# A decoder layer on one core: low halves of the weights from ACT and an accumulating DMA

## The chip, the core and the metric

The kernel runs on one core of a Trainium2 chip. The core has a matrix engine (TensorE: PE for its matmuls, PEld for its weight loads), a vector engine (VectorE: DVE), a scalar engine (ScalarE: ACT), a general engine (GpSimd: POOL), an engine for synchronisation (SyncE: SP), and 16 DMA engines. Each engine has its own queue of instructions and works through it in order; between engines there are semaphores. Matmuls write to PSUM, of which this kernel uses eight banks; all else on chip lies in SBUF.

The metric is the device time of one execution in microseconds (us), the median of the runs.

## What is computed

One layer of a decoder, for 8 batches of 100 tokens of width 1024, in float32: a retention over the own tokens, an attention over 722 context tokens and the own ones, and a gated feed-forward, each followed by a residual sum and a layer norm.

```python
x = _layernorm(x + _L0_attn_ref(x, Wq, Wk, Wv, Wg, Wo, g_norm_weight))
x = _layernorm(x + _L0_xattn_ref(x, ctx_2048, wq, wk, wv, wo, wk_ctx, wv_ctx, q_norm_w, k_norm_w))
x = _layernorm(x + _L0_ffn_ref(x, w_gate, w_up, w_down))

# _L0_attn_ref: 8 heads, keys of 128, values of 256
q, k, v, g = hidden @ Wq, hidden @ Wk, hidden @ Wv, hidden @ Wg        # q and k then with rotary factors
scores = einsum('bihd,bjhd->bhij', q * scale, k) * D[None]             # D: decay, causal
o = einsum('bhij,bjhd->bihd', scores, v)
o = o * rsqrt(mean(o * o) + EPS) * g_norm_weight * (g * sigmoid(g))
return o.reshape(B, T, H * DV) @ Wo

# _L0_xattn_ref: 16 heads of 128, 4 kv heads
q, k, v = x @ wq, x @ wk, x @ wv                                       # q, k normed, then rotary factors
# keys and values of the context in front of the own ones, softmax, then @ wo

# _L0_ffn_ref
return (silu(x @ w_gate.T) * (x @ w_up.T)) @ w_down.T
```

## The kernel before

**Products.** A product in float32 is made of three fast passes. Each operand is split into a high half, which is the operand rounded to the 12 significant bits that one pass takes, and a low half, which is what is left: `split2` (L68 to L70) does it with a copy by ACT into the type float32r (L69, CAST in the profile) and a subtraction by DVE (L70). `mm3` (L87 to L90) then issues three matmuls of 128 x 128 weights on 400 tokens: high by high, high by low, low by high. So nearly all of PE's work stands on L88, L89 and L90.

**Weights.** `load_w` (L72) loads a block of weights [128, 1024] (8 k tiles of 128 x 128, 512 KB) into one of three staging buffers `wst` by a DMA that SP issues (L78), and splits it into one of four buffers `w`. One such block gives 24 matmuls for each half of the tokens. A staging buffer may be loaded again when DVE's subtraction has read it; a buffer `w` may be written again when PE is done with it.

**Stages.** The tokens are worked on in two halves of 4 batches (400 tokens).

1. Retention (first attention), head by head: projections, scores, o, gate; the result goes to DRAM (`o1d`).
2. `out_proj` (L208) with `wo1`, for each half: loads the half's o from DRAM into four tiles `big` (L387 in `load_o1`), then for eight blocks of rows and two parts of the 2048 rows of weights, `load_w(w[m, c])` (L220) and 24 matmuls; adds the residual `rs` (L228, L231), and norms the half (`norm_root`, `norm_early`, `norm_late`, `scaled`; the result is stored to `zd`, L265). The four tiles of one half take the place of those of the other half.
3. Queries, keys and values of the own tokens for the second attention, called here the second retention projections (the loop over `kv`): for each of 4 kv heads six blocks of weights (four of queries, one of keys, one of values), in groups of two (four and two for the first head), `ws = [load_w(w2[kv, i]) ...]`, each used for both halves. Of each product of q or k, ACT makes the squares (L414), POOL sums them over the partitions (`partition_all_reduce`, L125), ACT and DVE make the inverse root (`inv_root`, L112 to L120), DVE applies the rotary factors to PSUM (`rope`, L134 to L137) and the root (L419), ACT and DVE split the result `d`, and SP stores it (`qd`, `kd`, L423; `vd`, L411). The bank of PSUM is free when rope has read it.
4. Second attention, per batch and kv head, with context projections, scores, softmax (two more `partition_all_reduce`, `mb`) and o (`o2d`).
5. `out_proj` with `wo2`, again for two halves.
6. Feed-forward, by seven instead of eight products of blocks.

**Order.** The tile framework orders the instructions of each engine by a model of their times and puts in the semaphores; buffers of a pool are taken in turn, and a writer waits for the last reader of its buffer. So the order on each queue follows from the program and that model, not from the text alone.

**What the change touches.** `load_w` as called in `out_proj` (64 blocks: 2 halves x 8 x 2, in two stages) and in the loop over `kv` (24 blocks). The names above are those of the profile's lines: `w<-wst` is the split of a block of weights, `wst<-in_wo` the load of a block of Wo or wo, `wst<-in_w` that of the other weights, `ss<-sq` the all-reduce of the squares, `big<-o1d` and `big<-o2d` the loads of o.

Of the kernel before, what the change touches and what calls it, by code (L numbers as in the profile page):

```python
# [8 lines left out]
F32 = mybir.dt.float32  # L9
FR = mybir.dt.float32r  # L10
AF = mybir.ActivationFunctionType
ALU = mybir.AluOpType
# [4 lines left out]
P = 128  # L17
B, T, D = 8, 100, 1024
NB = 4                 # batches in a half
N = NB * T             # tokens in a half  # L20
KT = D // P            # k tiles of the model width
QT = KT // 2           # k tiles in one of the four big tiles
SC, SH = 722, 362      # context tokens per batch, and in the first half of it
SN = [SH, SC - SH]
NC = 7                 # chunks of keys: SC of the context, then T own ones
ORDER = (6, 5, 0, 1, 2, 3, 4)
C5 = SC - 5 * P        # context keys in chunk 5
R6 = SC + T - 6 * P    # keys in chunk 6
T6 = T - R6            # first token that sees keys of chunk 6
N6 = 4 * R6            # scores of chunk 6, of the tokens that see its keys  # L30
NH1 = 8                # heads of the first attention
NKV = 4                # kv heads of the second
NHID = 32              # blocks of the hidden width
UNITS = NHID // 2      # pairs of hidden blocks
LAST = 3               # pairs of the last down projection
CUT = 5 * T            # tokens in the first of the two parts that are normed last
# [5 lines left out]
def decoder_layer(ctx, tc, xT, cT, w1, wo1, w2, wo2, wc, w3, wd, gw, qw, kw, trig, dec, mask, out):  # L42
# [21 lines left out]
    def split(dst, src):  # L64
        """dst[:, 0] + dst[:, 1] == src, each with the 12 significant bits that one pass takes."""
        split2(dst[:, 0], dst[:, 1], src)
# [5 lines left out]
    def load_w(src, w=None, parts=1):  # L72
        st = wp.tile([P, KT * P], F32, tag="wst", name="wst", bufs=3)
        if w is None:
            w = wp.tile([P, 2, KT * P], FR, tag="w", name="w", bufs=4)
        for i in range(parts):
            c = slice(i * KT * P // parts, (i + 1) * KT * P // parts)
            nc.sync.dma_start(out=st[:, c], in_=src[:, c])  # L78
            split(w[:, :, c], st[:, c])
        return w  # L80
# [30 lines left out]

    def inv_root(pool, ss, eps, n=N):  # L112
        """-2 (ss + eps)^-1/2: by exp(-ln/2), then a Newton step."""
        r = pool.tile([P, n], F32, tag="r0", name="r0")
        nc.scalar.activation(r, ss, AF.Ln, bias=eps)  # L115
        nc.scalar.activation(r, r, AF.Exp, scale=-0.5)  # L116
        q = pool.tile([P, n], F32, tag="r1", name="r1")
        nc.scalar.activation(q, r, AF.Square)
        nc.vector.scalar_tensor_tensor(q, ss, eps, q, ALU.add, ALU.mult)  # L119
        nc.vector.scalar_tensor_tensor(q, q, 3.0, r, ALU.subtract, ALU.mult)  # L120
        return q
# [6 lines left out]
    def rope(pool, acc, cosw, sinw, tag="t1"):  # L128
        """acc * cos + (acc with its halves swapped) * sin."""
        t1 = pool.tile([P, N], F32, tag=tag, name=tag)  # L130
        t2 = pool.tile([P, N], F32, tag="t2", name="t2")
        a = bt(acc)
        h = P // 2
        nc.vector.tensor_tensor(bt(t1), a, cosw[:, None, :].to_broadcast([P, NB, T]), ALU.mult)  # L134
        nc.vector.tensor_tensor(bt(t2[0:h]), a[h:P], sinw[h:P, None, :].to_broadcast([h, NB, T]), ALU.mult)
        nc.vector.tensor_tensor(bt(t2[h:P]), a[0:h], sinw[0:h, None, :].to_broadcast([h, NB, T]), ALU.mult)  # L136
        nc.vector.tensor_tensor(t1, t1, t2, ALU.add)  # L137
        return t1

    def tokens_first(pool, acc):  # L140
        """[128, 4 x 100] -> PSUM [100, 4 x 128]: the transposes of the four batches."""
        vt = pool.tile([P, N], F32, tag="vt", name="vt", bufs=1)
        nc.scalar.copy(vt, acc)
        tr = bank("s")
        for b in range(NB):
            nc.tensor.transpose(tr[0:T, b * P:(b + 1) * P], vt[:, b * T:(b + 1) * T], ident)
        return tr[0:T]

# [1 line left out]
    o1d = dr.tile([NH1, P, 2, 2, 2, N], FR, name="o1d")            # head, p, half, block, hi/lo, token  # L150
# [42 lines left out]
    def load_constants(p, trg):  # L193
        dcy = p.tile([T, NH1, T], F32, name="dcy", bufs=1)
        nc.sync.dma_start(out=dcy, in_=dec)
        nc.sync.dma_start(out=msk, in_=mask)
        nc.sync.dma_start(out=wts[:, 0:2], in_=gw)
        nc.sync.dma_start(out=wts[:, 2:3], in_=qw)
        nc.sync.dma_start(out=wts[:, 3:4], in_=kw)
        # rotary tables with the norm weights of q and k; factors left over from inv_root  # L200
        nc.vector.tensor_scalar(gws, wts[:, 0:2], -8.0, None, ALU.mult)
        nc.vector.tensor_scalar(kws, wts[:, 3:4], -0.5 * math.sqrt(P), None, ALU.mult)
        nc.vector.tensor_scalar(tq, trg[:, 2:4], wts[:, 2:3], None, ALU.mult)
        nc.vector.tensor_scalar(tk, trg[:, 2:4], wts[:, 3:4], None, ALU.mult)
        return dcy

# [1 line left out]
    def out_proj(half, w, load_o, res, yp, ybufs, p, make_z, dst, after=None):  # L208
        """res + o @ w of one half, then its layer norm: split for the next products, and to dst."""
# [4 lines left out]
        for ms in [range(first)] + [[m] for m in range(first, KT)]:  # L214
# [3 lines left out]
            for c in range(2):  # L218
                for m, acc in zip(ms, accs):
                    wt = load_w(w[m, c])  # L220
                    for k in range(KT):
                        kt = c * KT + k
                        rh, rl = og(kt)
                        a = acc if len(rh.shape) == 2 else bt(acc)
                        mmw(a, wt, k, rh, rl, kt == 0, kt == 2 * KT - 1)
# [55 lines left out]
    # A norm with little left to do once the last block of rows is there: all blocks are taken relative to the mean  # L281
    # of the others, so that the mean of what they then hold, delta, is that of the last block alone, and the
    # variance is mean(y^2) - delta^2 (delta^2 is at most an eighth of mean(y^2)).
# [24 lines left out]
    with sbuf("l1", 2) as p:  # L308
# [17 lines left out]
        for h in range(NH1):  # L326
# [14 lines left out]
            # scores with their decay, and o^T  # L341
# [21 lines left out]
            # a block of the context weights, split once for all batches  # L363
# [33 lines left out]
    kapool = sbuf("ka", 2, "right")  # L397
    ka = kapool.__enter__()
    with sbuf("l2", 2) as p:
        for kv in range(NKV):  # L400
            for i0, i1 in ((0, 4), (4, 6)) if kv == 0 else ((0, 2), (2, 4), (4, 6)):
                ws = [load_w(w2[kv, i]) for i in range(i0, i1)]
# [24 lines left out]
    y2pool = sbuf("y2", 1)  # L427
    y2p = y2pool.__enter__()
    with sbuf("cx", 2) as p, sbuf("c1", 1) as p1:
        for b in range(B):  # L430
# [10 lines left out]
            for kv in range(NKV):  # L441
                # K^T of the context, to be scaled by its norms when the scores leave PSUM, and V
# [29 lines left out]
                # -2 / norm of the context keys, keys on partitions  # L472
# [14 lines left out]
                # scores, keys on partitions, and their maximum  # L487
# [23 lines left out]
                # exponentials, split, and their sum  # L511
# [27 lines left out]
                # 1 / sum: exp(-ln), then a Newton step (the sum is 1 or more)  # L539
# [22 lines left out]
    # [C11 C12; C21 C22] = [A11 A12; A21 A22] [B11 B12; B21 B22] by Strassen's seven products; the rows of A  # L562
    # are two blocks of one weight, the columns of B the two halves of the tokens
# [60 lines left out]
    def w_pair(*ops):  # L624
        """Two of the sums of quarters of a weight, split; a sum goes to the first quarter's place unless that is kept."""
# [15 lines left out]
    def seven(i, part, t0=None):  # L641
        """Two blocks of the gate (part 0) or of the other factor (part 1): C11, C12, C21, C22."""
# [19 lines left out]
        def add(t, x, y, op=ALU.add):  # L662
            nc.vector.tensor_tensor(t, x, y, op)  # L663
# [3 lines left out]
        add(s2, s2, s4)                                     # C21  # L667
# [6 lines left out]
        add(s4, s4, prod(t2, 1, "b11+b12"))                 # C22  # L674
        m5 = prod(t3, 0, "b22")
        add(s1, s1, m5, ALU.subtract)                       # C11
        add(s3, s3, m5)                                     # C12
        return s1, s3, s2, s4

    # the first two blocks by all eight products: half of them need the first half of the tokens alone  # L680
# [13 lines left out]
    with sbuf("ff", 1) as p:  # L694
# [59 lines left out]
        # the last rows are normed in two parts  # L754
# [16 lines left out]
def _chunks(w, n):  # L771
    """[K, M] -> [M / 128, K / (n 128), 128, n 128]: k tiles of 128 x 128 side by side."""
    import numpy as np
    K, M = w.shape
    a = w.reshape(K // (n * P), n, P, M // P, P)
    return np.ascontiguousarray(a.transpose(3, 0, 2, 1, 4)).reshape(M // P, K // (n * P), P, n * P)
# [62 lines left out]
```

## Time and profile before

| | us |
|---|---|
| median of 3 runs | 2617.55 |
| lowest and highest of them | 2616.77, 2619.95 |
| span of the profiled execution | 2615.0 |
| PE busy in it | 2552.7 |
| DVE busy | 1922.2 |
| ACT busy | 1256.3 |
| POOL busy | 466.3 |

The span runs from the first to the last instruction of one execution that the hardware profiler recorded; the median of the runs is 2.55 us above it. A matmul's record of some 340 ns overlaps the next one's; at full clock they start 0.18 us apart. The page's map of the span, in 40 slices of 65 us, has the busy share of a slice in tenths, the granted clock of PE and the share of the 16 DMA engines:

```profile
PE   8999999999998899999999999999999999999998
...
DVE  4454554456999888888988989866866766866885
ACT  4555544533555455655655566533433433423351
POOL 0010000000544434434333343100000000000000
PEclk9999999999999999999999999999999999999999
DMA  5323333664434644544554553564421211211221
```

The first out_proj is in slices 8 to 10 (counted from 1), the second retention projections in 11 to 14, the second out_proj in 26 to 28. In a row such as `L70 DVE TENSOR_TENSOR w<-wst,w 128x1024 ... x300 | 303.7, 1015` the numbers after the bar are the busy time of the group and the mean nanoseconds of one. In a list of waits, `PE a L88 <- DVE t L136: 22.9, 5, 7.1` says that PE, at matmuls of L88 into banks `a`, waited for DVE's instruction of L136, 22.9 us in total, five times, at most 7.1 us.

### The profile page before, as it was taken

The page shows a single profiled execution, that of the slowest core. Times are in us where ns is not written, and L with a number is a line of the kernel's source. Part 1 is how long each engine was busy: PE and PEld are TensorE (multiplying, and loading weights), DVE is VectorE, ACT ScalarE, POOL GpSimd, SP SyncE. Part 2 cuts the span into 40 slices and gives each one's busy share as a digit, 9 for nine tenths or more (in the row PEclk, how much of TensorE's full clock was granted, in tenths as well). Part 3 has the DMA queues.
Part 4 walks back from the last instruction along what each step waited for, and adds up shares of the span by engine and source line. Part 5 has one row for each costly group of instructions (what it writes and reads, how often), then busy time and mean ns, then how long its engine had stood idle before and what let it go on. Part 6 is the DMA issues. An engine that isn't in the chain of part 4 may idle for free.

```text
span 2615.0 us, 37589 instructions
## 1 busy us (share of the span) xinstructions
PE 2552.7 (98%) x14438; PEld 2511.4 (96%) x14438; DVE 1922.2 (74%) x3201; ACT 1256.3 (48%) x2202; POOL 466.3 (18%) x222
## 2 busy tenths in 40 slices
PE   8999999999998899999999999999999999999998
PEld 8999999999998899999999999999999999999996
DVE  4454554456999888888988989866866766866885
ACT  4555544533555455655655566533433433423351
POOL 0010000000544434434333343100000000000000
PEclk9999999999999999999999999999999999999999
DMA  5323333664434644544554553564421211211221
GB/s 173 98 98 119 100 117 122 214 241 154 144 133 138 236 158 137 188 158 146 174 166 139 185 173 113 210 245 143 146 73 65 73 57 65 81 50 64 70 84 51
DMA packets 157233, 346.44 MB, mean 132 GB/s; under 512 B 45018, under 2 KB 95578, under 8 KB 147838
## 3 DMA queue, kind: packets, MB, share of 16 engines
q1 hardware_dynamic: 157054, 344.05, 39.5%
q8 instruction: 113, 1.85, 0.3%
q14 instruction: 66, 0.54, 0.1%
HBM read 279.81 MB, written 64.19 MB: 132 GB/s over the span
## 4 chain that ended last, share of the span: by engine, by line
PE 80%; DVE 10%; ACT 6%; issue 3%; DMA 2%; SPq 0%; DVEq 0%; ACTq 0%
PE a L88 16%; PE a L90 16%; PE a L89 16%; PE s L88 8%; PE s L89 8%; PE s L90 8%; PE v L88 3%; PE v L90 2%; PE v L89 2%; DVE r L119 1%; ACT L116 1%; ACT L115 1%; PE s L469 1%; DVE ot L378 1%; DVE t L136 1%
## 5 line engine op out<-in xcount | busy, mean ns | idle before, releaser
L88 PE MATMUL a<-big,w 128*128 128x400 f32 (+2 forms) x2300 | 778.5, 339 | 17.1 <-ACT big L69 9.5
L89 PE MATMUL a<-big,w 128*128 128x400 f32 (+2 forms) x2300 | 779.7, 339 | 0.0
L90 PE MATMUL a<-big,w 128*128 128x400 f32 (+2 forms) x2300 | 778.3, 339 | 0.0
L88 PEld LDWEIGHTS a<-big,w 128*128 128x128 f32 x2300 | 432.4, 188 | 20.6 <-ACT big L69 9.8
L90 PEld LDWEIGHTS a<-big,w 128*128 128x128 f32 x2300 | 433.9, 189 | 0.6
L89 PEld LDWEIGHTS a<-big,w 128*128 128x128 f32 x2300 | 433.1, 188 | 1.1 <-DVE big L70 0.5
L69 ACT CAST w<-wst 128x1024 fp32r<-128x1024 f32 (+2 forms) x300 | 259.2, 869 | 346.6 <-PE a L90 152.6
L70 DVE TENSOR_TENSOR w<-wst,w 128x1024 fp32r<-128x1024 f32 (+2 forms) x300 | 303.7, 1015 | 164.8 <-ACT w L69 163.2
L125 POOL PARTITION_ALL_REDUCE ss<-sq x56 | 157.3, 2817 | 725.4 <-DVE sq L362 442.3
L459 POOL PARTITION_ALL_REDUCE kss<-ksq x64 | 171.6, 2682 | 141.2 <-ACT ksq L458 140.7
L69 ACT CAST w<-as 128x512 fp32r<-128x512 f32 x90 | 55.9, 621 | 215.3 <-PE a L90 180.9
L88 PE MATMUL s<-big,w 128*128 128x400 f32 x428 | 150.4, 352 | 2.5 <-ACT big L69 2.5
L89 PE MATMUL s<-big,w 128*128 128x400 f32 x428 | 149.4, 349 | 1.6 <-DVE big L70 1.6
L90 PE MATMUL s<-big,w 128*128 128x400 f32 x428 | 148.8, 348 | 0.0
L505 ACT ACTIVATE s<-s,rk 128x400 f32<-128x400 f32 x160 | 88.0, 591 | 97.3 <-DVE sm L527 63.3
L663 DVE TENSOR_TENSOR s<-s 128x400 f32<-128x400 f32 x183 | 102.4, 569 | 25.3 <-ACT s L659 19.5
L125 POOL PARTITION_ALL_REDUCE mb<-sm x32 | 83.3, 2603 | 201.1 <-DVE sm L527 201.1
L524 ACT ACTIVATE s<-s 128x800 f32<-128x800 f32 (+1 forms) x128 | 95.1, 750 | 41.0 <-DVE s L518 38.1
L70 DVE TENSOR_TENSOR pl<-s,ph 128x800 fp32r<-128x800 f32 (+1 forms) x128 | 108.3, 850 | 2.5 <-ACT ph L69 2.0
L506 DVE TENSOR_TENSOR mx<-mx,s 128x400 f32<-128x400 f32 x128 | 80.5, 629 | 26.5 <-ACT s L505 23.3
L88 PE MATMUL a<-z,w 128*128 128x400 f32 x192 | 70.5, 367 | 24.0 <-DVE t L136 22.9
L69 ACT CAST ph<-s 128x800 fp32r<-128x800 f32 (+1 forms) x128 | 92.4, 731 | 0.9
(269 smaller groups left out, 5605.6 us busy)
## 6 DMA issues: line engine op xcount, KB each, us to landing
wst<-in_w SPq DMA_DIRECT2D x137, 512.0 KB
w<-wcd SPq DMA_DIRECT2D x64, 1024.0 KB
wst<-in_wo SPq DMA_DIRECT2D x64, 512.0 KB
wst<-in_wd SPq DMA_DIRECT2D x32, 512.0 KB
o1d<-of SPq DMA_DIRECT2D x32, 400.0 KB
big<-o1d SPq DMA_DIRECT2D x16, 800.0 KB
qd<-d SPq DMA_DIRECT2D x32, 400.0 KB
q<-qd SPq DMA_DIRECT2D x32, 400.0 KB
```

The costliest lines, as they stand in the source:

```text
L69: nc.scalar.copy(hi, src)
L70: nc.vector.tensor_tensor(lo, src, f32(hi), ALU.subtract)
L88: nc.tensor.matmul(acc, lh, rh, start=start, stop=False)
L89: nc.tensor.matmul(acc, lh, rl, start=False, stop=False)
L90: nc.tensor.matmul(acc, ll, rh, start=False, stop=stop)
L115: nc.scalar.activation(r, ss, AF.Ln, bias=eps)
L125: nc.gpsimd.partition_all_reduce(y, x, P, op)
L459: nc.gpsimd.partition_all_reduce(ss[:, at], sq[:, at], P, RED.add)
L505: nc.scalar.activation(sc, sp, AF.Copy, scale=rk[:, c:c + 1])
L506: nc.vector.tensor_tensor(mx, s[:, 1] if j == 2 else mx, sc, ALU.max)
L524: nc.scalar.activation(e, e, AF.Exp)
L663: nc.vector.tensor_tensor(t, x, y, op)
```

## The change

A second loader, `load_wa`, takes the place of `load_w` in `out_proj` and in the loop over `kv`. SP loads the staging buffer as before, and ACT makes the high half. Then ACT writes the negated high half where the low half is to be, and a DMA issued by POOL adds the staging buffer to it: low = -high + weight. DVE has no part in it. `load_w` stays for all other weights. The rest of the diff takes out comments and docstrings; the new function moves the lines behind it down by ten.

```diff
+    def load_wa(src):
+
+        st = wp.tile([P, KT * P], F32, tag="wst", name="wst", bufs=3)
+        w = wp.tile([P, 2, KT * P], FR, tag="w", name="w", bufs=4)
+        nc.sync.dma_start(out=st, in_=src)
+        nc.scalar.copy(w[:, 0], st)
+        nc.scalar.activation(w[:, 1], f32(w[:, 0]), AF.Copy, scale=-1.0)
+        nc.gpsimd.dma_start(out=f32(w[:, 1]), in_=st, accum_op=ALU.add)
+        return w
+
...
     def out_proj(half, w, load_o, res, yp, ybufs, p, make_z, dst, after=None):
...
-                    wt = load_w(w[m, c])
+                    wt = load_wa(w[m, c])
...
         for kv in range(NKV):
             for i0, i1 in ((0, 4), (4, 6)) if kv == 0 else ((0, 2), (2, 4), (4, 6)):
-                ws = [load_w(w2[kv, i]) for i in range(i0, i1)]
+                ws = [load_wa(w2[kv, i]) for i in range(i0, i1)]
```

## The prediction

> **What bounds the kernel now.** I read the page's engine rows first, then PE's waits stage by stage, then the stretches of time in which the changed loads stand. PE is the bound almost everywhere.
>
> ```profile
> span 2615.0 us, 37589 instructions
> PE 2552.7 (98%) x14438; PEld 2511.4 (96%) x14438; DVE 1922.2 (74%) x3201; ACT 1256.3 (48%) x2202; POOL 466.3 (18%) x222
> ```
>
> So only what makes PE wait counts. The first out_proj begins near 505 us, the second retention projections run from about 655 to 875, and the second out_proj from about 1685 to 1820. PE's waits from 500 to 880 us:
>
> ```profile
> PE a L88 <- DVE t L136: 22.9, 5, 7.1
> PE s L270 <- DVE s L245: 1.4, 1, 1.4
> PE a L88 <- ACT w L69: 1.1, 1, 1.1
> ...
> ```
>
> The reader is to see that DVE holds PE for 22.9 us in all, always by rope's last read of a PSUM bank (L136). Five stretches of that stage, then four of the two out_proj stages (us; busy PE, PEld, DVE, ACT, POOL; granted clock; DMA share; GB/s):
>
> ```profile
> 680.00:710.00 30.00, 25.26 (x127) 24.52 (x126) 29.62 (x53) 16.91 (x33) 14.92 (x6) 0.89 0.40 135
> 710.00:740.00 30.00, 30.00 (x167) 30.00 (x166) 29.52 (x44) 15.79 (x31) 16.12 (x6) 1.00 0.38 135
> 740.00:770.00 30.00, 27.36 (x146) 26.91 (x145) 29.71 (x47) 16.79 (x32) 11.37 (x5) 0.94 0.37 125
> 800.00:830.00 30.00, 22.94 (x115) 22.46 (x114) 29.61 (x46) 15.97 (x30) 12.52 (x5) 0.83 0.39 134
> 870.00:886.00 16.00, 9.20 (x39) 9.12 (x40) 14.84 (x29) 8.56 (x18) 7.81 (x3) 0.79 0.38 147
> ...
> 510.00:520.00 10.00, 9.88 (x55) 9.54 (x55) 2.45 (x2) 2.54 (x3) 0.00 (x0) 1.00 0.98 350
> 525.00:555.00 30.00, 30.00 (x168) 30.00 (x167) 12.86 (x16) 7.36 (x7) 0.00 (x0) 1.00 0.51 165
> 565.00:580.00 15.00, 13.63 (x74) 13.30 (x74) 12.40 (x20) 7.08 (x11) 0.00 (x0) 1.00 1.02 416
> 1730.00:1748.00 18.00, 16.72 (x88) 16.09 (x88) 13.64 (x21) 7.12 (x12) 0.00 (x0) 1.00 1.03 407
> ```
>
> In the projections DVE is full (29.5 to 29.7 of 30 us), and after each wait the granted clock falls too. In out_proj it is the reverse: DVE is under half busy in 525 to 555 and PE loses nothing there, but the DMA engines are full at the start of the stage (0.98) and where one half's o gives way to the other's (1.02, 1.03). Two more views: ACT and SP in time order.
>
> ```profile
> 512.77 1.05 ACT L69 CAST w<-wst 128x1024 fp32r<-128x1024 f32 x1 [1.98 <-DMA wst<-in_wo]
> 519.31 1.05 ACT L69 CAST w<-wst 128x1024 fp32r<-128x1024 f32 x1 [5.49 <-DMA wst<-in_wo]
> 521.64 1.05 ACT L69 CAST w<-wst 128x1024 fp32r<-128x1024 f32 x1 [1.29 <-PE a L90]
> 525.99 1.05 ACT L69 CAST w<-wst 128x1024 fp32r<-128x1024 f32 x1 [3.30 <-PE a L90]
> ```
> ```profile
> 509.44 2.97 SPq L78 DMA_DIRECT2D wst<-in_wo  x2
> ...
> 528.34 0.33 SPq L78 DMA_DIRECT2D wst<-in_wo  x1
> ```
>
> A weight lasts PE 4.35 us (521.64 to 525.99). The load issued at 509.44 was used at 512.77: 3.3 us. Its successor, issued at 512.08, was used at 519.31: 7.2 us, in the full stretch. The cast of 525.99 lets wst be loaded again at 528.34, 2.35 us later.
>
> **The change, part by part.** 88 weights change: 2 halves x 8 x 2 in each out_proj (64) and 4 x 6 in the projections.
>
> *Taken from DVE:* 88 subtractions (L70, 128x1024). Their groups by stage have 1221 ns in out_proj and 1443 ns in the projections: 64 x 1.22 + 24 x 1.44 = 113 us. In out_proj that is idle time of DVE made longer, worth nothing: PE covers it there. In the projections it is 35 us of a full engine. What PE loses there, against the 167 matmuls of the undisturbed row, clock included: (167-127) + (167-146) + (167-115) matmuls of 0.18 us, and 50 in 870 to 886 (89 fit into 16 us): 7.2 + 3.8 + 9.4 + 9.0 = 29 us. That is the ceiling of the gain. Its floor is zero, as these weights now come later and may be waited for instead of DVE. I take 12: the new way of a weight goes through POOL, whose queue in this stage also has 40 all-reduces of 2.85 us and waits for ACT and DVE in turn.
>
> *Added to ACT:* 88 negations of 128x1024. The cast of this size has 1.05 us; 92 us in all. ACT's rows (7.4 of 30, 17 of 30 us) hide them; each is 1.05 us on the way of its weight.
>
> *Added to POOL:* 88 DMA issues, in order with the all-reduces. In the changed order two stand ahead of the last head's two all-reduces, 20 between those of the projections, 10 among the last softmax reductions. Each waits for its negation, and that for PE to release a w buffer; behind it stand all-reduces whose results ACT (L115) and then DVE (L119) wait for. No POOL DMA is in the trace: the price of an issue lies between SP's 0.33 us and the 2.85 us of an all-reduce. I take 0.33, as the same kind of row; 24 of them are 8 us of a stage in which POOL is idle half the time, nothing on the path. At 2.85 they would fill 68 us of it and eat the gain of 12.
>
> *Added to the DMA engines:* 88 moves of 512 KB that read two operands and write one. At the full rows' 416 GB/s one pass of 512 KB keeps all engines for 1.27 us. Bounds: one pass (1.27, as a plain copy) and three (3.8: read, read, write each at full price); I take two (2.54), both reads passing where one did. In the even part of out_proj the engines are busy 0.51 x 4.35 = 2.2 us per weight; with 2.54 that is 4.75 against PE's 4.35, an excess of 0.4; by the 0.45 share of another even stretch (610 to 628 us), 0.15. Of the 64 weights some 48 lie in such stretches: 7 to 19 us, I take 13. The other 16 lie in the full stretches, four to five in each of 510-520, 565-580 and 1730-1748 with what leads to them: 4.6 x 2.54 = 12 us of transfers with no room, beside the o1d and o2d tiles that PE needs next. Some of it falls behind the need, but a PE wait here brings the slow clock too (0.83 above): I take 10 us for each, 30 (bounds: 0, as landings may have slack, and 17 each at three passes).
>
> *Moved on SP:* the reload of wst waited for DVE's subtraction, 2.35 us after the cast began; now for the accumulating DMA: 1.05 + 1.05 + 0.33 + 3.3 (the load's own time) + 1.27 (second pass) = 7.0 us. With the load itself 10.3 us for three wst buffers that must turn round in 3 x 4.35 = 13.0 us: it holds in the even part, and not with a load of 7.2 us. Behind the waiting reload on SP stand rs, the o tiles and zd. At the change of halves the new order has two wst loads ahead of the eight zd stores, not three, and those stores wait for the norm; so one weight less is in hand there. Price 0 (if the buffers in hand cover it) to 10 us (a load's 3.3, two ACT passes, the accumulation's 4.9, for each half change); I take 5 for each out_proj, 10.
>
> *The Trainium skill.* "DMA: Bandwidth & Descriptors", "Issuing engines are not separate DMA queues", says that DMAs issued from several engines run on the same 16 DMA engines and interleave. That speaks against this change; the rows at 1.02 show these engines full, and if POOL's were separate, the 13 and 30 would vanish and the time be about 2616. The same page ("Anatomy of one DMA — SWDGE (gpsimd) path") fits a POOL DMA as 2.0 us + bytes / 436e3 per us: 3.2 us for 512 KB, an estimate that knows no second read; by it the round of wst is 9.0 us, and only the 10 would shrink. No row here shows a POOL DMA.
>
> **Sum** against the profiled execution: 2615.0 - 12 + 13 + 30 + 10 = 2656. The median of the runs is 2617.55, 2.55 above that span, so 2658.6; I say **2658**. With the bounds that stay at two passes (gain 29 to 0, even part 7 to 19, full stretches 15 to 36, SP 0 to 20) it is 2611 to 2692.
>
> **Rivals.**
> 1. *The accumulation is dearer (three passes, 3.8 us).* Then out_proj is DMA-bound throughout: 2.2 + 3.8 = 6.0 us per weight, 1.65 over PE's, x 48 = 79; the full stretches 3 x 17 = 51; no gain in the projections: 2617.55 + 130 = 2748. For it: there is no spare time at 1.02. Against it: reads and the write may overlap.
> 2. *Faster: DVE's relief decides.* If an accumulation costs one pass, the even part needs 2.2 + 1.27 = 3.5 of 4.35 us and stays hidden, and the tiles' landings have slack. Then the gain of the projections stands nearly alone, 22 of the 29 less 7 at the full stretches: 2603. It decides as soon as an accumulation takes under about 2 us of the engines. For it: DVE is full where PE waits. Against: the row at 510 us, in which PE already loses 0.12 us for a late o tile.
> 3. *Gain and loss cancel.* One pass, with 12 us gained and as much lost at the stretches: 2617. That the change does not do what it says is excluded: in the changed order DVE has no w subtraction left in these stages.
>
> **How the numbers follow.** Chances: the forecast 0.60, rival 1 0.22, rival 2 0.09, rival 3 0.09. What can be told from no change is 0.2%, 5 us. Faster 0.09, same 0.09, slower 0.82. The range takes in rival 3 and the lower part of rival 1 (0.60 + 0.09 + about 0.14): 2612 to 2760.
>
> **What will show it.** PE's waits for DVE t L136 fall from 22.9 to under 12 us; new waits of PE for w (by ACT or a DMA) and for big<-o1d appear at both changes of halves; the DMA share is near 1 through out_proj; SP's wst loads wait for the accumulating DMA. I am wrong if the granted clock stays 1.00 through both out_proj stages, if that share stays under 0.8, or if the projections alone lengthen.

## The result, and the profile after

The changed kernel takes 2686.07 us (median of 4 runs, 2685.14 to 2693.0) against 2617.64 us for the kernel before, measured beside it. The ratio is 1.0265, with a 95% interval of 1.025 to 1.0279: slower by 2.65%. The profiled execution of after has a span of 2683.9 us, 68.9 us more than that of before.

From the page of after: the span, the engines' busy times, and the rows of the new DMA (its issue on POOL, and its way from issue to landing).

```profile
span 2683.9 us, 37816 instructions
PE 2571.2 (96%) x14438; PEld 2518.5 (94%) x14438; DVE 1827.3 (68%) x3113; ACT 1342.1 (50%) x2290; POOL 543.3 (20%) x310
...
L89 POOL DMA_DIRECT2D w<-wst x88 | 77.0, 875 | 373.2 <-ACT w L88 330.3
...
w<-wst POOLq DMA_DIRECT2D x88, 512.0 KB, 6.4
```

DVE has lost 94.9 us of work, and the kernel is slower all the same. PE has the same 14438 matmuls. It is busy 18.5 us longer (the mean granted clock is 0.985, before 0.992) and idle 50.4 us longer. An issue takes 0.875 us on POOL; the median accumulation lands 6.4 us after its issue.

PE's waits from 500 to 920 us (engine and line, what it waited for, us in total, times, longest); the lines of before are now ten further down, so L98 is the first matmul of `mm3`, L100 the one that reads the low half, and L146 rope's last read:

```profile
PE a L98 <- DVE t L146: 15.4, 4, 5.1
PE a L98 <- ACT w L87: 10.8, 3, 8.7
PE s L98 <- DMA big<-o1d: 10.0, 5, 4.7
PE a L100 <- DMA w<-wst: 6.9, 6, 2.4
PE s L100 <- DMA w<-wst: 6.3, 3, 2.7
```

The old wait fell from 22.9 to 15.4 us. Below it stand three other kinds, 34.0 us in all where before had 1.1 (the cast, L69): for the cast of a weight that came late, for the other half's o, and, at L100, for the accumulation itself.

Stretches of after (us; busy PE, PEld, DVE, ACT, POOL; granted clock; DMA share; GB/s):

```profile
510.00:520.00 10.00, 7.22 (x39) 6.56 (x38) 0.00 (x0) 2.11 (x2) 0.84 (x1) 1.00 1.04 316
525.00:555.00 30.00, 27.63 (x142) 26.67 (x140) 4.60 (x8) 11.97 (x13) 5.12 (x6) 0.94 0.93 235
580.00:600.00 20.00, 9.37 (x32) 6.68 (x30) 9.11 (x17) 9.58 (x14) 2.58 (x3) 0.78 1.04 325
750.00:780.00 30.00, 30.00 (x168) 29.95 (x167) 29.59 (x50) 22.46 (x41) 20.25 (x11) 1.00 0.68 190
...
1780.00:1800.00 20.00, 14.02 (x48) 11.94 (x49) 7.80 (x16) 8.27 (x14) 0.86 (x1) 0.68 1.04 347
```

In 525 to 555, where before had 168 matmuls at a DMA share of 0.51, there are 142 at 0.93, and fewer GB/s than a share of 0.98 had before (235 against 350): the engines are busy with more than the bytes that are counted. The worst rows are the changes of halves. In 580 to 600 PE does 32 matmuls; 111 fit into 20 us at 0.18 us apart, so 79 x 0.18 = 14 us are lost, 10.6 of them idle and the rest at the slower clock (0.78 in this row). The projections (750 to 780) still have DVE full.

Numbering the matmuls of both traces by their start gives the delay at each mark. What each stage added or took off:

| stage (times of before, us) | matmuls | predicted | measured |
|---|---|---|---|
| start of the first out_proj, 500 to 520 | 2847 to 2954 | +10 | +10.4 |
| changes of halves, 566 to 600 and 1734 to 1780 | 3201 to 3383, 9772 to 10014 | +30 (20, and 10 for SP) | +20.4 + 17.8 = +38.2 |
| even parts, 520 to 566, 600 to 643, 1780 to 1813 | the rest of out_proj | +13 | +5.5 + 12.5 + 9.4 = +27.4 |
| projections, 643 to 900 | 3612 to 4849 | -12 | -9.5 |
| all else | | 0 | +2.4 |
| span | | +41 | +68.9 |

The even parts deserve a closer look. ACT, POOL and SP of after in order of time (start, duration, engine, line, operation; in brackets the idle time before and what ended it):

```profile
533.81 1.05 ACT L87 CAST w<-wst 128x1024 fp32r<-128x1024 f32 x1 [8.14 <-DMA wst<-in_wo]
535.86 1.04 ACT L87 CAST w<-wst 128x1024 fp32r<-128x1024 f32 x1
537.89 1.03 ACT L87 CAST w<-wst 128x1024 fp32r<-128x1024 f32 x1
549.72 1.05 ACT L87 CAST w<-wst 128x1024 fp32r<-128x1024 f32 x1 [9.70 <-DMA wst<-in_wo]
...
536.25 0.86 POOL L89 DMA_DIRECT2D w<-wst  x1 [9.43 <-ACT w L88]
...
541.42 3.13 SPq L86 DMA_DIRECT2D wst<-in_wo  x2
```

Weights come in bursts of three, one for each staging buffer, and then nothing for 9.7 us. One round of a buffer: cast at 533.81, accumulation issued at 536.25 (2.4 us), buffer loaded again at 541.42 (5.2 us), next cast at 549.72 (8.3 us): 15.9 us for three weights, of which PE uses three in 13.0.

### The profile page after: what moved, and what is told of

It reads as the page before. It is cut to its first block, busy times and chain, and to the rows that moved or that the text cites. A ratio compares the mean times of both kernels' runs of the same rounds, so it can differ in the third digit from the quotient of the medians.

```text
span 2683.9 us, 37816 instructions
## 1 busy us (share of the span) xinstructions
PE 2571.2 (96%) x14438; PEld 2518.5 (94%) x14438; DVE 1827.3 (68%) x3113; ACT 1342.1 (50%) x2290; POOL 543.3 (20%) x310
## 4 chain that ended last, share of the span: by engine, by line
PE 67%; DMA 13%; DVE 9%; ACT 5%; issue 5%; SPq 0%; POOL 0%; DVEq 0%; POOLq 0%; ACTq 0%
PE a L98 13%; PE a L99 13%; PE a L100 13%; PE s L98 6%; PE s L99 6%; PE s L100 6%; DMA wst<-in_wo 5%; DMA w<-wst 4%; PE v L98 2%; PE v L100 2%; PE v L99 2%; DMA wst<-in_w 1%; DVE r L130 1%; DVE r L129 1%; DMA cs<-in_cT 1%
## 5 line engine op out<-in xcount | busy, mean ns | idle before, releaser
L98 PE MATMUL a<-big,w 128*128 128x400 f32 (+2 forms) x2300 | 780.2, 340 | 24.2 <-ACT big L69 9.2
L100 PE MATMUL a<-big,w 128*128 128x400 f32 (+2 forms) x2300 | 780.3, 340 | 8.1 <-DMA w<-wst 8.1
L98 PEld LDWEIGHTS a<-big,w 128*128 128x128 f32 x2300 | 433.4, 189 | 29.1 <-ACT big L69 9.5
L100 PEld LDWEIGHTS a<-big,w 128*128 128x128 f32 x2300 | 434.9, 189 | 11.7 <-DMA w<-wst 11.1
L70 DVE TENSOR_TENSOR w<-wst,w 128x512 fp32r<-128x512 f32 (+2 forms) x212 | 191.4, 905 | 122.6 <-ACT w L69 121.5
L69 ACT CAST w<-wst 128x512 fp32r<-128x512 f32 (+2 forms) x212 | 167.0, 795 | 204.0 <-issue 95.6
L98 PE MATMUL s<-big,w 128*128 128x400 f32 x428 | 155.4, 364 | 21.9 <-DMA big<-o1d 10.0
L87 ACT CAST w<-wst 128x1024 fp32r<-128x1024 f32 x88 | 92.0, 1046 | 158.6 <-DMA wst<-in_wo 130.2
L69 ACT CAST w<-as 128x512 fp32r<-128x512 f32 x90 | 55.9, 621 | 212.7 <-PE a L100 180.9
L100 PE MATMUL s<-big,w 128*128 128x400 f32 x428 | 151.5, 355 | 6.3 <-DMA w<-wst 6.3
L99 PE MATMUL s<-big,w 128*128 128x400 f32 x428 | 152.3, 356 | 1.7 <-DVE big L70 1.7
L89 POOL DMA_DIRECT2D w<-wst x88 | 77.0, 875 | 373.2 <-ACT w L88 330.3
L98 PEld LDWEIGHTS s<-big,w 128*128 128x128 f32 x428 | 83.8, 196 | 29.7 <-DMA big<-o1d 11.3
```

The costliest lines, as they stand in the source:

```text
L69: nc.scalar.copy(hi, src)
L70: nc.vector.tensor_tensor(lo, src, f32(hi), ALU.subtract)
L87: nc.scalar.copy(w[:, 0], st)
L89: nc.gpsimd.dma_start(out=f32(w[:, 1]), in_=st, accum_op=ALU.add)
L98: nc.tensor.matmul(acc, lh, rh, start=start, stop=False)
L99: nc.tensor.matmul(acc, lh, rl, start=False, stop=False)
```

## The experiments

Theory A: the round of the staging buffers sets the pace of out_proj. Theory B, the prediction's: the accumulation's two passes fill the DMA engines. The table has the us that each run's profile adds to the kernel before in each part of out_proj, and in the projections, by the same matmuls as above; the medians of the runs follow below. Each column is one profiled execution, so a difference of a few us says nothing. The columns are named as the runs are below.

| | after | out_only | wst4 | edges | one_pass | tiny | load | hold |
|---|---|---|---|---|---|---|---|---|
| start | 10.4 | 10.9 | 9.4 | 5.6 | 9.0 | 3.9 | -0.4 | -0.4 |
| changes of halves | 38.2 | 39.8 | 33.0 | 6.5 | 24.5 | 5.8 | 11.2 | 26.4 |
| even parts | 27.4 | 26.5 | 0.9 | 8.6 | 0.3 | 0.0 | 11.3 | 17.9 |
| out_proj in all | 76.0 | 77.2 | 43.3 | 20.7 | 33.8 | 9.7 | 22.1 | 43.9 |
| projections | -9.5 | 2.5 | -5.3 | -2.8 | -14.6 | -13.0 | 2.1 | -11.0 |

### Each part alone: kv_only and out_only

```diff
-                    wt = load_wa(w[m, c])       # kv_only: old load in out_proj
+                    wt = load_w(w[m, c])
```
```diff
-                ws = [load_wa(w2[kv, i]) for i in range(i0, i1)]     # out_only: old load in the projections
+                ws = [load_w(w2[kv, i]) for i in range(i0, i1)]
```

> The new load is kept in the second retention projections alone (24 weights); both out_proj have the old load, with the subtraction on DVE. Theory (all of the loss lies in out_proj, the projections gained 9.5 us between their first and last marks): 2617.6 - 10 = about 2607 us (2603 to 2612), and PE's waits for rope's last read (L146) near 15 us as in the changed kernel, not 22.9. Rival (the projections only looked shorter because they began late and their first weights had been prefetched against a held-up PE): no gain, 2615 to 2622 us. Rival 2 (the POOL queue with all-reduces and accumulations in turn costs time of its own): slower than 2622 us.

Measured: 2610.32 us, ratio 0.9968 (0.9957 to 0.998). In the range, and faster than before. PE's waits for rope's last read are 15.8 us, as announced.

> The new load is kept in the two out_proj alone (64 weights); the projections have the old load. Theory (stages add up): 2617.6 + 78 = about 2695 us (2688 to 2702): first out_proj +48, second +27 to +30. Rival (the two parts share a cost, such as POOL's queue from one stage into the next): 2670 to 2685 us, under what the changed kernel takes, since the accumulations of the projections would then be part of the cause.

Measured: 2697.39 us, ratio 1.0303 (1.0289 to 1.0317). In the range. So the parts add up to within a few us: out_proj costs some 79 us, the projections give back 8 (kv_only) to 11 (out_only less after).

### How much lies in the bytes: one_pass and tiny

```diff
-        nc.gpsimd.dma_start(out=f32(w[:, 1]), in_=st, accum_op=ALU.add)
+        nc.gpsimd.dma_start(out=f32(w[:, 1]), in_=st)                                          # one_pass
+        nc.gpsimd.dma_start(out=f32(w[:, 1, 0:8]), in_=st[:, 0:8], accum_op=ALU.add)           # tiny
```

Both leave out what the low half needs (one_pass all of the subtraction, tiny that of 1016 of 1024 columns) and serve for the time alone.

> All 88 weights as in the changed kernel, but POOL's DMA copies the staging buffer into the low half instead of adding it: the subtraction is left out (the low half holds the weight itself), everything else stays, the wait for the negation and the landing too. One pass of the DMA engines for each weight instead of two. Theory B (engine load decides): in the even part 2.2 + 1.27 of 4.35 us, no excess, and the full stretches at half price: 2625 to 2640 us. Theory A (round of the staging buffers: only the second pass, 1.3 us of some 15.7 for three weights, and what the landing gains under less load, comes off): 2645 to 2670 us.

Measured: 2636.32 us, ratio 1.0071 (1.0056 to 1.0086). That is in theory B's range and under theory A's. One pass less is worth 49.8 us of the median, 42.2 of them in out_proj.

> All 88 weights take the changed way (cast and negation on ACT, then a POOL DMA that adds), but the DMA adds 8 of the 1024 columns only, so 4 KB instead of 512 KB: the subtraction of the other columns is left out (there the low half holds the negated high half). Order, waits and the POOL queue stay, the bytes go. Theory D (the loss is the bytes: engine time of the accumulations and the landings that they lengthen, on a round with too few buffers): out_proj as before, the projections gain 10 to 15 us: 2602 to 2610 us. Rival E (the longer way itself, with its negation, its issue and the fixed part of a landing, and the staging loads that SP sends later for it): the start of the first out_proj still loses some 9 us as with one pass, the changes of halves some 5 each, 2617.6 + 19 - 15 = 2618 to 2632 us.

Measured: 2613.61 us, ratio 0.9985 (0.9976 to 0.9994): between the two ranges. Out_proj still loses 9.7 us with next to no bytes: that is the longer way itself (issue and landing; the negation alone costs nothing, as neg_dve shows below), at the start and the changes of halves. So out_proj loses 9.7 us with 4 KB for a weight, 33.8 with one pass of 512 KB, 76.0 with two.

What a pass is, by the DMA queues from 525 to 555 us (packets, MB, share of the 16 engines' time), POOL's queue being q0. After, then one_pass:

```profile
q0 software_dynamic: 842, 3.06, 55.6%
```
```profile
q0 software_dynamic: 1069, 3.92, 35.5%
```

For 512 KB (0.524 MB) that is 0.556 x 30 x 0.524 / 3.06 = 2.86 us of all engines for an accumulation, and 0.355 x 30 x 0.524 / 3.92 = 1.42 us for a copy: two passes, as the prediction took it, each some 12% dearer than its 1.27 us. (Over the whole of each profiled execution the same sum gives 2.87 and 1.35 us, so the factor is good to some 6%.)

### Load on the engines, and a held buffer: load and hold

Both keep the old load and the subtraction on DVE; the projections have the old load too.

```diff
+        w = load_w(src)                          # hold: load_w's lines written out, as st is needed here
+        for c in range(2):
+            d = dr.tile([P, KT * P], F32, tag="spare", name="spare", bufs=8)
+            nc.gpsimd.dma_start(out=d, in_=f32(w[:, 0]))                   # load
+            nc.gpsimd.dma_start(out=d, in_=st)                             # hold, in its place
```

> Both out_proj with the old load and its subtraction on DVE; beside each of the 64 weights two POOL DMAs of 512 KB store its high half into DRAM, where nothing reads it. That is the DMA load of two passes for each weight, and a w buffer is held until they land, but no staging buffer waits for it and no weight waits for POOL. The projections have the old load. Theory B (full DMA engines are the cause): 2680 to 2700 us, as out_proj alone with the new load. Theory A (the round of the staging buffers): most of the loss is gone, 2620 to 2645 us, with the DMA share as high as in the changed kernel.

Measured: 2634.38 us, ratio 1.0064 (1.005 to 1.0078): theory A's range. The row of load for the even part (columns as above):

```profile
525.00:555.00 30.00, 25.41 (x127) 25.06 (x126) 12.14 (x14) 7.34 (x7) 7.37 (x14) 0.89 1.03 412
```

The engines are as full as in any row here (1.03), fuller than in after (0.93), and yet the run loses 22.1 us in out_proj, not 76. That this row has fewer matmuls than after's (127 for 142) comes from one wait of 4.6 us, of PE for a residual sum of DVE (`y`), and the slower clock (0.89): the run loses 10.9 us in this even part and 0.4 in the other two together. So full engines alone, in transfers that no weight waits for, explain some 22 of the 76 us.

> As the run that only added DMA load to out_proj (old load, and two POOL DMAs of 512 KB for each weight that write to DRAM, where nothing reads; 2634.4 us), but the two DMAs read the staging buffer instead of the finished weight. The DMA load is the same; what is new is that a staging buffer is held until both have landed. No weight waits for POOL. Theory A (a held staging buffer costs time of its own, since loads then come in bursts of three): clearly over 2634.4, 2650 to 2690 us. Theory C (holding it costs little; what costs is that PE itself must wait for the low half to land on the weight's own path): 2630 to 2642 us.

Measured: 2646.04 us, ratio 1.0111 (1.0096 to 1.0126): under theory A's range and over theory C's. In out_proj hold loses 43.9 us, 21.8 more than load, with the same DMAs: that is the price of a staging buffer that is held until they land (in load it is the buffer `w` that is held). The rest up to 76.0, 32.1 us, is left for what only after has, above all that PE may not use a weight until its own DMA has landed; no run takes that alone. These are differences between runs whose effects feed each other, so a rough division.

### One staging buffer more: wst4 and before_wst4

```diff
-        st = wp.tile([P, KT * P], F32, tag="wst", name="wst", bufs=3)
+        st = wp.tile([P, KT * P], F32, tag="wst", name="wst", bufs=4)
...
-        s1 = p.tile([P, N], F32, tag="s1", name="s1", bufs=2)
+        s1 = p.tile([P, N], F32, tag="s1", name="s1", bufs=1)
...
-                s3 = p.tile([P, y.shape[2]], F32, tag="s2", name="s2", bufs=2)
-                nc.vector.tensor_tensor(s3, s2, sq, ALU.add)
-                s2 = s3
+                nc.vector.tensor_tensor(s2, s2, sq, ALU.add)      # s2: a buffer of its own, bufs=1
```

> The changed kernel with four staging buffers for weights instead of three (the room comes from the norm's sums of squares, which go into one buffer instead of two, and s1, one instead of two). Theory A (the round of the staging buffers sets the pace: load, cast, negation, issue and landing in turn, three weights in 15.5 to 15.9 us where PE uses three in 13.0): a fourth buffer gives 17.3 us for the same round, so that the even part of out_proj is nearly restored and only the full stretches stay: 2635 to 2655 us. Theory B (the second pass of the accumulation fills the 16 DMA engines, as the prediction had it): a buffer more does not change what they must move: 2678 to 2690 us.

Measured: 2665.61 us, ratio 1.0195 (1.0177 to 1.0212). Outside both ranges in total, in which some 8.5 us are the last norm's (the control below loses them too). By stages it tells more. Two rows of wst4, and PE's wait for the o tiles in its first out_proj:

```profile
525.00:555.00 30.00, 29.70 (x165) 29.37 (x164) 5.17 (x9) 14.77 (x14) 5.56 (x7) 1.00 1.03 265
566.00:600.00 34.00, 22.28 (x97) 19.66 (x96) 10.18 (x19) 12.80 (x18) 3.44 (x4) 0.80 1.04 331
...
PE s L98 <- DMA big<-o1d: 9.6, 3, 7.1
```

The even parts are whole again: 165 matmuls for after's 142, and 0.9 us lost for 27.4, at a DMA share of 1.03. So what after lost there was lost by the round of three buffers. That round is long because the engines are loaded: in one_pass, with three buffers and one pass, three weights take 10.5 to 13.1 us from cast to cast in 520 to 566 us, and the even parts lose 0.3 us. One pass less or one buffer more removes the loss. The changes of halves (566 to 600) are nearly as bad as in after (33.0 us for 38.2).

This does not clear the DMA engines. In wst4 their share is 1.02 over the whole first out_proj (501 to 673 us; 0.64 in before, 501 to 643), and SP issues the loads of the other half's o later: five of them between the matmuls 2954 and 3201, where before has eight. So theory B may hold for the 43.3 us that wst4 still loses in out_proj, at the start and the changes of halves.

> The kernel before with the fourth staging buffer and the smaller norm buffers of the earlier run, no other change: the control for it. If the buffers alone are worth nothing, 2615 to 2622 us, and the 20 us that the fourth buffer took off the changed kernel belong to the accumulation's round; if the kernel before gains as well (2600 to 2612), part of them does not.

Measured: 2613.7 us, ratio 0.9986 (0.9976 to 0.9995): between its two cases. No part of out_proj changes (0.0 to 0.1 us in each), so the 26.5 us of the even parts belong to the accumulation's round. The control gains 6.5 us in the projections and 5.3 in 1830 to 1900 us, and loses 8.6 us in the last norm, where single squares lost their second buffer.

### Accumulations beside the o tiles: edges

```diff
+                    i += 1                                   # counts the weights of one half
+                    edge = i <= 4 or (half == 0 and i > 12)
-                    wt = load_wa(w[m, c])
+                    wt = (load_w if edge else load_wa)(w[m, c])
```

> As the run with four staging buffers (2665.6 us), but the first four weights of each half of both out_proj and the last four of the first half (24 of 64, those beside the o tiles' loads) have the old load with DVE's subtraction; 40 of out_proj's weights and the 24 of the projections keep the accumulation. Theory (with a fourth buffer, what is left is lost where accumulations compete with big<-o1d and big<-o2d at the start and the change of halves): 2615 to 2640 us, and PE's wait for big<-o1d falls from 9.6 us to under 4. Rival (it is lost evenly, each accumulated weight costing (2665.6 - 2607) / 64 = 0.9 us): 2607 + 40 x 0.9 = 2643 us or more, the wait for big<-o1d as before.

Measured: 2646.56 us, ratio 1.0114 (1.0095 to 1.0132). The total is outside the theory's range and in the rival's; the stages and waits say otherwise. PE's waits in edges from 500 to 700 us:

```profile
PE a L100 <- DMA w<-wst: 9.3, 3, 4.1
...
PE s L282 <- DVE s L258: 1.4, 1, 1.4
PE a L98 <- ACT w L87: 1.1, 1, 1.1
```

There is no wait for `big<-o1d` left (9.6 us in wst4), nor one for `big<-o2d` in the second out_proj (10.2 us in wst4), and the changes of halves lose 6.5 us for 33.0: the o tiles were late because accumulations stood beside their loads. In place of it PE waits three times for a low half, where the accumulated weights begin again; the even parts lose 8.6 us for 0.9. So the theory was right on the place and blind to the new transitions; a mixed loader gains 19 us on wst4 and stays 29 us slower than the kernel before.

### ACT's negation alone: neg_dve

```diff
-        nc.gpsimd.dma_start(out=f32(w[:, 1]), in_=st, accum_op=ALU.add)
+        nc.vector.tensor_tensor(w[:, 1], st, f32(w[:, 1]), ALU.add)
```

> All 88 weights with cast and negation on ACT, but DVE adds the staging buffer to the negated half, instead of POOL's DMA: the new load without its DMA. It keeps ACT's 88 negations of 1.06 us on each weight's way and DVE's full work. If ACT's step is hidden, as the prediction had it: 2615 to 2624 us. If it costs by itself in the projections (DVE as full as before, and the weights later): 2624 to 2640 us.

Measured: 2612.94 us, ratio 0.9981 (0.9972 to 0.999), 2 us under the range of the first case; out_proj -0.1 us. The negations cost nothing. The 4.9 us by which this run's median lies under the kernel before, with as much work on DVE, lie in the projections (-4.3): so much comes from another order of the work alone. The part on the prediction takes this up.

### A version that beats both: kv4, and its control b4

```diff
-                s2 = p.tile([P, y.shape[2]], F32, tag="s2", name="s2", bufs=1)
+                one = len(ms) == 1
+                s2 = p.tile([P, y.shape[2]], F32, tag="sq" if one else "s2", name="s2", bufs=2 if one else 1)
```

This goes on top of the four staging buffers; kv4 has the new load in the projections alone, b4 nowhere.

> A version that may beat both kernels: the new load in the projections alone (2610.3 us), with four staging buffers and the smaller norm buffers (before with them: 2613.7 us), and two buffers kept for the single squares of the last norm, where the control lost 8 us. If the gains add up: 2618 - 8 - 4 - 8 = 2598 us; if buffers and accumulation gain the same 7 us of the projections: 2603 to 2608 us.

Measured: 2606.12 us, ratio 0.9953 (0.9939 to 0.9966): the second case. It is the fastest kernel of this study: 11.7 us under the kernel before, of which the control shows 5.0 to come from the buffers.

> The kernel before with the same buffers as the run beside it, and no accumulation at all: the control that tells what the accumulation itself is worth there. 2605.5 us if the last norm gets its 8 us back (2603 to 2609); the accumulation in the projections is worth the difference between the two runs, 0 to 8 us.

Measured: 2612.84 us, ratio 0.9979 (0.997 to 0.9988), 7 us over the value expected, though the last norm has its 8.6 us back (the delay is -8.1 us before it and after it). Its profiled execution, with a span of 2606.9 us, lies at the low end of its runs (2608.71 to 2616.23), so the marks of one execution are good to a few us only. Between the two medians lie 6.7 us for the new load in the projections, and the intervals do not touch.

## Why the prediction was right, and which terms were not

*Direction and mechanism.* Slower by out_proj, with the projections giving back too little: shown by out_only and kv_only. The time, 2686.07, lies in the range, 28 us over the forecast. The range (2612 to 2760) is wide, so this says little; the places of the losses say more. By the table the forecast was too low by 14.4 us in the even parts, 8.2 at the changes of halves, 2.5 in the projections, 0.4 at the start and 2.4 elsewhere: nothing cancelled. Two numbers of the working do not follow from it: the lower bound of 15 for the full stretches, where the text above it has 0, and 4.6 weights for each of three stretches, where 16 weights make 5.3.

*Accumulation, two passes:* right, 2.86 against 1.42 us for a copy. Rival 1 (three passes), rival 2 and rival 3 (one pass) fall with it; rival 2's faster kernel doesn't appear at one pass either (2636.32).

*Start of the first out_proj, 10:* 10.4, by luck. It was put down to two passes in full engines, but one_pass loses 9.0 there and tiny 3.9: the longer way and the first pass make nearly all of it.

*Even part, 13:* 27.4, and the reason was wrong. The prediction put an excess of DMA engine time there (4.75 us for a weight against 4.35) and let the staging round pass: "it holds in the even part", 10.3 of 13.0 us. This step failed. The round took 15.9 us: to the issue 2.4 (predicted 2.4), accumulation 5.2 (4.6), and the next load 8.3 us where the prediction had kept the 3.3 us of an undisturbed load. Loads and accumulations come three at a time and share the engines (0.93 in 525 to 555), so they are slow, and the buffer is held through both. With a fourth buffer the even parts lose 0.9 us, with one pass less 0.3. So the excess of engine time that the prediction put here costs nearly nothing here, even at wst4's share of 1.03; what it costs at the changes of halves was not taken alone.

*Changes of halves, 20 and 10 for SP:* 38.2. The place and the mechanism are right (edges takes 33.0 to 6.5 us by keeping accumulations away from the o tiles), the size is short by 8. Which part of it is SP's was not taken alone.

*POOL's issue, 0.33:* 0.875 us. Issue and landing together, with hardly any bytes, cost 9.7 us in out_proj (tiny), none of it in the even parts. *ACT's negation, hidden:* right (neg_dve).

*Projections, -12:* -9.5 in this profile. PE's wait for rope fell to 15.4 us, not under 12 as announced. How much of it is the accumulation's merit can't be read from one profile: with the old load there, the stage took +2.5 (out_only), +2.1 (load), -2.4 (b4), -6.5 (before_wst4) and -11.0 us (hold) against before, presumably by the order that the weights and the all-reduces fell into. The medians give 7.7 us for the new load there (kv_only against before) and 6.7 (kv4 against b4). But neg_dve, with all of DVE's work, is 4.9 us under the kernel before, and kv_only only 2.6 us under neg_dve; how much of the 7 us is DVE's relief and how much the new order stays open. DVE, at 29.59 of 30 us in 750 to 780, is as full as before in that stretch, but not in all: in kv_only's 820 to 850 it has 25.39 (before 29.72). Between the marks 3612 and 4849 its busy time falls from 247.1 us in before to 229.0 in kv_only, and its idle time grows from 9.7 to 20.9, while the stage gains 6.9. So the ceiling of 29 us was not in reach of 24 subtractions; the last section has one reason, and no run takes it alone.

*Signs announced:* waits for w and for the o tiles (big<-o1d at the first change of halves, big<-o2d at the second), the share near 1 and SP's waits for the accumulating DMA (33.5 us of SP in 525 to 566, for DVE's subtraction 18.5 before) all came.

The Trainium skill's page "DMA: Bandwidth & Descriptors" ("Anatomy of one DMA — SWDGE (gpsimd) path") gives an estimate of 3.2 us for 512 KB issued by POOL. The plain copies of one_pass have a median of 3.7 us in 700 to 960 us, at a DMA share of 0.61, and 4.8 in 480 to 700, at 0.77, so it is near for a copy where the engines have room. The accumulations of after have 5.8 and 6.7 us in these stretches (shares 0.72 and 0.93), which the fit doesn't cover.

## What to carry to other kernels

When work moves from an engine to a DMA, follow the buffer that the DMA reads: its round is load, passes, issue and landing, all at the durations of the loaded engines, and it must be shorter than (number of buffers) x (use time): here 15.9 us against 3 x 4.35 = 13.0. With full DMA engines, transfers that nobody waited for cost 22 us in out_proj (load), those on the way of the next operand 76 (after). Place such a DMA only in stages where the engine to be relieved is full and the DMA engines are not: here in 24 weights of 88, worth 0.3%, of which a part may be the new order of the queues.

## What the hardware showed beyond that

An accumulating DMA from SBUF to SBUF took the engines about twice the time of a copy (2.86 against 1.42 us for 512 KB), and an issue of it 0.875 us of POOL (after), a copy's 0.537 (one_pass).

In the projections DVE is partly full because POOL runs beside it. DVE and POOL of kv_only in order of time:

```profile
750.61 2.11 DVE L147 TENSOR_TENSOR t<-t,t 128x400 f32<-128x400 f32 x1
...
768.03 0.57 DVE L147 TENSOR_TENSOR t<-t,t 128x400 f32<-128x400 f32 x1
...
750.31 2.85 POOL L135 PARTITION_ALL_REDUCE ss<-sq  x1 [2.43 <-DVE r L129]
```

The same sum of two tiles in SBUF takes 0.57 us alone and 2.11 us when an all-reduce has just begun; it ends at 752.72, shortly before the all-reduce does (753.16). The Trainium skill's page "SBUF — State Buffer" ("Who interferes with whom") says that a DVE instruction with two inputs in SBUF contends with a GpSimd instruction that reads SBUF; this pair agrees with it. Rope's three instructions, which read a PSUM bank, take 0.57 us with an all-reduce beside them or without. Added up between the marks 3612 and 4849, against the median of the same instruction without an all-reduce beside it, DVE's instructions take an estimated 31 us longer in before and 34 in kv_only. So this share of DVE's busy time is waiting, and taking the subtractions from DVE did not shorten it.
